# Projecting queries and keys for a later pair among the inner layers instead of among the exponentials, in an attention and feed-forward kernel on one NeuronCore

## The chip, the core and the metric

The kernel runs on one core of one Trainium2 chip. The metric is the time of one execution on the device in microseconds (us), lower is better. The figure shown for the kernel before is the median of three runs. TensorE is called PE here, VectorE DVE, ScalarE ACT, GpSimd POOL and SyncE SP, as in the profile.

## The reference

One transformer layer over 32 sequences of 256 tokens with 128 features, all in float32. Attention has 16 heads of 8 features, a causal mask and a distance penalty on the scores; the feed-forward part has hidden width 512 and weights that are small integers times a scale.

```python
Q, K, V = (split_heads(x @ W.T + b) for W, b in ((Wq, bq), (Wk, bk), (Wv, bv)))
scores = einsum('bhid,bhjd->bhij', Q, K) / sqrt(8)
scores = where(j > i, -inf, scores - (i - j))
attn = softmax(scores) @ V                       # heads joined again
x = layernorm(x + attn @ Wo.T + bo)
h = silu((x @ w1.T) * s1) * ((x @ w2.T) * s2)    # 128 -> 512
h = gelu((h @ h1.T) * sh1)                       # 512 -> 512
h = gelu((h @ h2.T) * sh2)                       # 512 -> 512
x = layernorm(x + (h @ w3.T) * s3)               # 512 -> 128
```

## The kernel before

Two sequences, 512 tokens, make a pair, and 16 pairs (0 to 15) go through the kernel one after the other. The program is a software pipeline, written out by hand: Python generators are advanced one step at a time, and the order in which their steps are called is the order of the instructions on PE, DVE, ACT and SP. The wrapper `InOrder` keeps that order, so that nearly all instructions of these engines carry its line, L58. POOL's instructions have lines of their own.

`step(n)` is iteration n. It has two stages.

**The loop** (L733 to L752) has twelve rounds. In each, `weigh(n, i)` computes one group of transposed scores of pair n on PE (tile `s`, two blocks of 512 columns in PSUM), ACT takes their exponential (`e`), and POOL zeroes what lies above the diagonal (L463). `row_maxima(n + 1, i)` computes the same kind of scores for the next pair, adds the mask with four small products, and DVE reduces them to row maxima (`m`), which that pair's exponentials will subtract. Every third round is a "diagonal" one with smaller blocks (`s_0d` to `s_3d`). Between the rounds stand steps of other work: the second half of pair n-2's last layer (`last`: tiles `pw`, `yT`, `py`, `y`, `z`), the products of exponentials and values (`outputs`: `pa`, `pt`), the transpose of pair n-1's normalized rows (`turn`: `px1T`), and, up to the change, the projection of pair n+2.

**The feed** (L793 to L795) is the feed-forward part of pair n-1: four blocks of the first layer (`pw`, Silu), then four blocks of each inner layer, `podd` and `peven`, with Gelu. The products of an inner layer come in three groups: sixteen for blocks 0 and 1, eight for block 2, eight for block 3. Hidden values are kept as a rounded part and a rest, each multiplied separately, so ACT takes each Gelu twice (`heven`, then `evenw`), and DVE subtracts the one from the other. For the last block of the second inner layer DVE copies instead. `feed` yields twelve times, each time between the products of a block and its activations, and at each yield the generator `rest()` does one step of other work: the last `outputs`, `maxima_to_rows`, `project_values`, the output projection (`finish`: `pon`, `onT`, `po`) and two layer norms. What is left of `rest()` when `feed` ends is run behind it (L795).

**The projection**, `project(n)`, has three steps. The first issues the load of the next pair's `x`, transposes this pair's rows on PE (`pxT`, four transposes), copies them to SBUF on DVE (`xT`) and adds the output bias to `x` on POOL (L325). The second multiplies by the query weights (`pq`), and `halves` writes a rounded part on ACT (`qhi`, Identity) and the rest on DVE (`qlo`). The third does the same for the keys (`pk`, `khi`, `klo`). The tiles qhi, qlo, khi and klo have one buffer each. At the end of the loop `stack(n + 2, ...)` copies them by DMA into the stacked operands `qs` and `ks`.

What sets the order around the change:

- Score tiles `s`, and the layers' `pw`, `podd` and `peven` in the feed, come from one pool of three PSUM buffers (L283); `pxT`, `pq`, `pk` and the other small products share two PSUM buffers of another pool (L284).
- The exponential, Silu and Gelu need different tables on ACT: `prepare` makes ACT load one ahead of its use, three times an iteration. The one for Exp stands at the end of the feed (L616).
- `late` holds the last step of `last(n - 2)`, the second norm's output and its store, and runs in round 3 of the next loop (L738).

Of the kernel before, what the change touches and what calls it, by code (L numbers as in the profile page):

```python
# [42 lines left out]
NPAIR = B // 2  # L43
# [18 lines left out]
def tile_attn_ffn(  # L62
# [39 lines left out]
    def load_x(n):  # L102
        t = xin[n % 4]
        sp.dma_start(out=t, in_=xv[n])
        return t
# [53 lines left out]
    def prepare(func):  # L159

        act.activation(nothing, half[:, 0:1], func)
# [124 lines left out]
    def work(nm):  # L286
        return ps_w.tile([P, 512], F32, name=nm, tag="work")
# [7 lines left out]
    def halves(n, ps, bias, nm):  # L295
        pool = setup if n == 1 else hlp
        hi = pool.tile([P, TOK], F32R, name=f"{nm}hi_{n}", tag=f"{nm}hi")
        act.activation(hi, ps, AF.Identity, bias=bias)
        lo = pool.tile([P, TOK], F32R, name=f"{nm}lo_{n}", tag=f"{nm}lo")
        vec.scalar_tensor_tensor(  # L300
            lo, ps, bias, hi.bitcast(F32), ALU.add, ALU.subtract
        )
        return hi, lo
# [10 lines left out]
    def project(n):  # L314
        xn = xs[n]
        if n + 1 < NPAIR:
            xs[n + 1] = load_x(n + 1)
        pt = work(f"pxT_{n}")
        for t in range(NT):
            pe.transpose(pt[:, t * P : (t + 1) * P], xn[:, t, :], ident)  # L320
        xT = xtp.tile([P, TOK], F32, name=f"xT_{n}", tag="xT", bufs=2)
        vec.tensor_copy(xT, pt)

        for t in range(NT):
            nc.gpsimd.tensor_tensor(xn[:, t, :], xn[:, t, :], bo_sb, ALU.add)  # L325
        yield
        pq = work(f"pq_{n}")
        pe.matmul(pq, lhsT=wq_sb, rhs=xT, start=True, stop=True)
        q = halves(n, pq, bq_sb, "q")
        yield  # L330
        pk = work(f"pk_{n}")
        pe.matmul(pk, lhsT=wk_sb, rhs=xT, start=True, stop=True)
        k = halves(n, pk, bk_sb, "k")
        m = mp.tile([P, 2, 2, H], F32, name=f"m_{n}", tag="m")
        pairs[n] = dict(
            q=qs[n % 2], k=ks[n % 2], qs=q, ks=k, m=m, xT=xT, xb=xs.pop(n)
        )
# [192 lines left out]
    def first_norm(n):  # L530
        x1 = x1s[n % 3]
        yield from layernorm(pairs[n]["xb"], x1, f"a_{n}")
        pairs[n] = dict(x1=x1)
# [4 lines left out]
    def turn(n, exact):  # L538
        pt = work(f"px1T_{n}")
        for t in range(NT):  # L540
            pe.transpose(pt[:, t * P : (t + 1) * P], pairs[n]["x1"][:, t, :], ident)
        x1T = xtp.tile([P, 2, TOK], F32R, name=f"x1T_{n}", tag="x1T")
        if exact:
            act.copy(x1T[:, 0, :], pt)
            vec.tensor_tensor(x1T[:, 1, :], pt, x1T[:, 0, :].bitcast(F32), ALU.subtract)
        else:
            x1T = x1T.bitcast(F32)
            vec.tensor_copy(x1T[:, 0, :], pt)
        pairs[n]["x1T"] = x1T
# [72 lines left out]
    def inexact_weights():  # L622

        found = const.tile([P, 11], F32, name="found")
        at = 0
        for nm, *_ in layers:
            rows = [t[nm].rearrange("p k o -> p (k o)") for t in (loaded, near)]
            for c in range(0, rows[0].shape[1], HID):
                whole, part = (t[:, c : c + HID] for t in rows)
                act.copy(part, whole)  # L630
                differ = once.tile([P, HID], F32, name=f"differ_{at}", tag="differ")
                vec.scalar_tensor_tensor(
                    differ, whole, 1.0, part.bitcast(F32), ALU.mult, ALU.not_equal,
                    accum_out=found[:, at : at + 1],
                )
                at += 1
                yield
        ones_col = const.tile([P, 1], F32, name="ones_col")
        nc.gpsimd.memset(ones_col, 1.0)
        count = work("pcount")  # L640
        pe.matmul(count[0:1, 0:11], lhsT=ones_col, rhs=found, start=True, stop=True)
        total = const.tile([1, 1], F32, name="total")
        vec.tensor_reduce(total, count[0:1, 0:11], AX.X, ALU.add)
        number = const.tile([1, 1], I32, name="number")
        vec.tensor_copy(number, total)
        pairs["inexact"] = number

    def last(n, exact, ws, gp):
        h = pairs[n]["h"]
        pT = work(f"pw3_{n}")  # L650
        for k in range(KC):
            parts = [h[:, i, k, :] for i in range(2 if exact else 1)]
            product(pT, ws["w3"][:, k, :], parts, k == 0, k == KC - 1)
        yT = gp.tile([P, TOK], F32, name=f"yT_{n}", tag="sg")
        act.activation(yT, pT, AF.Copy, scale=sc["s3"])
        yield
        po = work(f"py_{n}").rearrange("p (t d) -> p t d", d=D)
        for t in range(NT):
            pe.transpose(po[:, t, :], yT[:, t * P : (t + 1) * P], ident)
        y = yp.tile([P, NT, D], F32, name=f"y2_{n}", tag="y")  # L660
        z = yp.tile([P, NT, D], F32, name=f"z_{n}", tag="z")
        if n == NPAIR - 1:

            norms = []
            for t in (slice(0, NT // 2), slice(NT // 2, NT)):
                vec.tensor_tensor(y[:, t], po[:, t], pairs[n]["x1"][:, t], ALU.add)
                norms.append(layernorm(y[:, t], z[:, t], f"f_{n}_{t.start}"))
                next(norms[-1])
            for norm, t in zip(norms, (slice(0, NT // 2), slice(NT // 2, NT))):
                run(norm)  # L670
                sp.dma_start(out=ov[n][:, t], in_=z[:, t])
            return
        vec.tensor_tensor(y, po, pairs[n]["x1"], ALU.add)
        yield
        yield from layernorm(y, z, f"f_{n}")
        sp.dma_start(out=ov[n], in_=z)
        del pairs[n]

    def run(gen):
        for _ in gen:  # L680
            pass


    ahead = project(0)
# [7 lines left out]
    ahead = project(1)  # L692
# [32 lines left out]
    def step(n, exact=None, ws=None, hp=None, gp=None):  # L725


        side = iter(())
        settling = (
            last(n - 2, exact, ws, gp) if n > 1 else first_norm(0) if n else inexact_weights()  # L730
        )
        ahead = project(n + 2) if n + 2 < NPAIR else iter(())
        for i in range(3 * G):  # L733
            weigh(n, i)
            j = i + {0: LEAD, 1: -LAG}.get(n, 0)
            if n + 1 < NPAIR and 0 <= j < 3 * G:
                row_maxima(n + 1, j)
            if i == 3 and late:  # L738
                run(late.pop())
            next(side, None)  # L740
            if n and i == 9:
                turn(n - 1, exact)
            if i in ((0, 2) if n > 1 else (0, 2, 4, 6)) if n else i < 11:
                next(settling, None)

            if i in ((3, 4, 5) if n == 1 else (1, 3, 5)):
                next(ahead, None)
            if i % 3 == 2:
                run(side)
                side = outputs(n, i // 3)  # L750
            if n == 0 and i == 3 * G - LEAD:
                maxima_to_rows(1)  # L752
        if n < 2:
            run(settling)
        run(ahead)
        if n + 2 < NPAIR:
            stack(n + 2, "q")
            stack(n + 2, "k", sp if n else act)


        def rest():
            for _ in range(3):
                next(side)
                yield
            if n == 1:
                for i in range(3 * G - LAG, 3 * G):
                    row_maxima(2, i)
                    yield
            if 0 < n < NPAIR - 1:
                maxima_to_rows(n + 1)  # L770
            run(side)
            yield
            if n + 2 < NPAIR:
                project_values(n + 2)
                yield
            last_steps = finish(n)
            next(last_steps)
            yield
            yield from last_steps
            if n:  # L780
                yield
                yield from first_norm(n)
            if n == NPAIR - 1:
                yield
                turn(n, exact)
            if n > 1:
                next(settling)
                late.append(settling)

        if n:  # L790
            prepare(AF.Silu)
        due = rest()
        for _ in feed(n - 1, exact, ws, hp, gp) if n else ():  # L793
            next(due, None)
        run(due)  # L795
# [85 lines left out]
```

## Time and profile before

| | |
|---|---|
| median of 3 runs | 823.32 us (823.05 to 824.74) |
| the profiled execution | 824.06 us, span 822.2 us, granted PE clock 0.98 |
| loop of iteration 6, 318.45 to 341.72 us | 23.27 us |
| feed of iteration 6, 341.72 to 365.86 us | 24.14 us |
| busy share of the span | PE 95%, DVE 77%, ACT 64%, POOL 32% |

The profile is one execution taken by the hardware profiler; its times count from the start of its span. A row names an engine, an operation, its output and inputs by the program's names, and its duration; the time that an engine sat idle ahead of an instruction stands in brackets with what ended it. PE and ACT instructions are pipelined: the next one can start before the last has ended, so work is best measured from start to start. The clock column is the share of full speed that was granted to PE.

### The profile page before, as it was taken

What the parts mean: (1) busy time and instruction counts of PE and PEld (TensorE: products, weight loads), DVE (VectorE), ACT (ScalarE), POOL (GpSimd) and SP (SyncE); (2) the same over time, 40 slices, a digit from 0 to 9 for tenths busy, and PEclk for the clock granted to TensorE, in tenths of its full rate; (3) what the DMA queues carried; (4) which work ended last, traced back from release to release, by engine and by line L of the source; (5) the groups of instructions that cost most, each with busy time, mean ns of one, the idle gap of its engine ahead of it and who ended that gap; (6) DMA issues with size and microseconds to landing.
All of it is one profiled execution on the core that took longest, in us unless ns stands there. A gap on an engine that the chain in (4) does not pass through costs nothing.

```text
span 822.2 us, 17431 instructions
## 1 busy us (share of the span) xinstructions
PE 784.6 (95%) x7046; PEld 555.8 (68%) x7046; DVE 636.0 (77%) x1247; ACT 527.5 (64%) x719; POOL 260.8 (32%) x341
## 2 busy tenths in 40 slices
PE   4896999999999999999999999999999999999994
PEld 2664676776767677676767767676767767666673
DVE  6786778877887887778788877888878787873674
ACT  5065556766666766766576676667666666758572
POOL 5033413333142333414232342424243231424211
PEclk9879999999999999999999999999999999999998
DMA  6824140403204140410404040130404022000001
GB/s 147 213 62 106 29 92 14 106 15 74 60 14 106 28 107 14 92 42 21 110 17 106 27 101 20 43 90 15 107 26 104 4 62 59 14 4 14 1 8 37
DMA packets 39898, 47.49 MB, mean 58 GB/s; under 512 B 3968, under 2 KB 21632, under 8 KB 39808
## 3 DMA queue, kind: packets, MB, share of 16 engines
q1 hardware_dynamic: 37152, 42.82, 22.0%
q10 hardware_dynamic: 2656, 3.48, 1.9%
q8 instruction: 57, 0.93, 0.5%
q14 instruction: 33, 0.27, 0.1%
HBM read 7.48 MB, written 4.19 MB: 14 GB/s over the span
## 4 chain that ended last, share of the span: by engine, by line
PE 83%; DVE 4%; ACT 3%; issue 1%; DMA 0%; POOL 0%; ACTq 0%; POOLq 0%; DVEq 0%
PE peven L58 14%; PE podd L58 14%; PE s L58 12%; PE pa L58 11%; PE pw L58 10%; PE s_2d L58 2%; PE s_3d L58 2%; PE po L58 2%; PE s_0d L58 2%; PE s_1d L58 2%; PE pt L58 2%; PE pv L58 2%; PE pk L58 2%; PE pq L58 2%; PE px1T L58 1%; PE py L58 1%
## 5 line engine op out<-in xcount | busy, mean ns | idle before, releaser
L58 DVE TENSOR_REDUCE m<-s 128x4 f32<-128x1024 f32 x128 | 155.5, 1218 | 14.6 <-PE s L58 13.3
L58 ACT ACTIVATE e<-s 128x1024 f32<-128x1024 f32 x128 | 130.7, 1022 | 44.2 <-PE s L58 34.2
L463 POOL TENSOR_SCALAR_AFFINE_SELECT e<-e 128x512 f32<-128x512 f32 x128 | 82.6, 646 | 218.5 <-ACT e L58 189.3
L58 PE MATMUL podd<-h,h_near 128*128 128x512 f32 x512 | 131.3, 403 | 1.0 <-DVE m L58 0.5
L58 PE MATMUL peven<-hodd,h_near 128*128 128x512 f32 x512 | 122.7, 396 | 0.0
L58 PEld LDWEIGHTS peven<-hodd,h_near 128*128 128x128 f32 x512 | 95.7, 187 | 23.4 <-DVE hodd L58 0.3
L58 PEld LDWEIGHTS podd<-h,h_near 128*128 128x128 f32 x512 | 91.8, 188 | 23.1 <-DVE h L58 3.2
L58 ACT ACTIVATE hodd<-podd,sh 128x512 fp32r<-128x512 f32 x64 | 44.0, 688 | 62.7 <-PE podd L58 62.6
L58 PE MATMUL pw<-x1T,w_near 128*128 128x512 f32 x256 | 75.6, 418 | 1.1 <-DVE h0w L58 1.1
L274 POOL TENSOR_TENSOR rsa<-rsa,half 128x4 f32<-128x4 f32 x16 | 16.3, 1018 | 176.7 <-DVE rsa L58 176.7
L58 DVE SCALAR_TENSOR_TENSOR h0w<-pw,s,sg 128x512 f32<-128x512 f32 x64 | 47.9, 748 | 30.4 <-ACT sg L58 30.4
L58 PEld LDWEIGHTS s<-qs,ks 64*128 64x128 f32 x512 | 38.9, 188 | 47.7 <-issue 34.1
L58 PE MATMUL pa<-e,vaug 128*32 128x256 f32 x1024 | 70.6, 389 | 0.0
L58 PE MATMUL s<-qs,ks 64*128 64x256 f32 x512 | 65.3, 335 | 0.6 <-ACT e L58 0.5
L58 DVE TENSOR_TENSOR heven<-evenw,heven 128x512 fp32r<-128x512 f32 x64 | 44.2, 692 | 26.6 <-ACT evenw L58 26.1
L58 ACT ACT_TABLE_LOAD x47 | 60.3, 1283 | 3.4 <-issue 2.6
L58 ACT ACTIVATE sg<-pw,s 128x512 f32<-128x512 f32 x64 | 43.7, 684 | 28.2 <-PE pw L58 27.9
L58 PE MATMUL s<-ks,qs 62*128 62x256 f32 x512 | 56.9, 302 | 2.4 <-ACT e_0d L58 1.8
L58 ACT ACTIVATE heven<-peven,sh 128x512 fp32r<-128x512 f32 x48 | 33.4, 696 | 39.8 <-PE peven L58 39.8
L58 PEld LDWEIGHTS pw<-x1T,w_near 128*128 128x128 f32 x256 | 43.4, 188 | 18.4 <-ACT nothing L58 5.8
L581 POOL TENSOR_TENSOR h<-h0w,h 128x512 fp32r<-128x512 f32 x31 | 40.0, 1291 | 43.5 <-DVE h L58 41.2
L58 DVE TENSOR_TENSOR hodd<-oddw,hodd 128x512 fp32r<-128x512 f32 x64 | 43.7, 684 | 10.0 <-ACT oddw L58 9.9
(147 smaller groups left out, 1418.1 us busy)
## 6 DMA issues: line engine op xcount, KB each, us to landing
qs<-qhi SPq DMA_DIRECT2D x32, 256.0 KB
qs<-qlo SPq DMA_DIRECT2D x32, 256.0 KB
ks<-khi SPq DMA_DIRECT2D x26, 256.0 KB
ks<-klo SPq DMA_DIRECT2D x26, 256.0 KB
x<-in_x_dram SPq DMA_DIRECT2D x16, 256.0 KB
out_dram<-z SPq DMA_DIRECT2D x15, 256.0 KB
ks<-khi ACTq DMA_DIRECT2D x6, 256.0 KB
ks<-klo ACTq DMA_DIRECT2D x6, 256.0 KB
```

The source lines that it names most:

```text
L58: return lambda *args, **kw: self.tc.keep_in_program_order(call(*args, **kw))
L274: nc.gpsimd.tensor_tensor(rs, rs, half[:, 0:NT], ALU.pow)
L463: nc.gpsimd.affine_select(out=on_diagonal, in_=on_diagonal, pattern=[[0, on_diagonal.shape[1]], [1, P]], base=0, channel_multiplier=-1, co ...
L581: (nc.gpsimd if o < (1 if final else 2) else vec).tensor_tensor(h[:, 1, o, :], whole, h[:, 0, o, :].bitcast(F32), ALU.subtract)
```

## The change

Pairs 0 to 3 are projected as before. For pairs 4 to 15 the three steps of the projection move out of the loop of iteration n (where pair n+2 was projected, in rounds 1, 3 and 5) and into the end of the feed of the iteration before: in `rest()` of iteration n, pair n+3 is projected. From iteration 2 to 12 the first step falls to the tenth yield of the feed, the second to the eleventh, none to the twelfth, and the third behind the feed. In iteration 1, where `rest()` is three steps longer, all three fall behind the feed. The loops of iterations 2 to 13 hold no projection any more. The stacking copies stay at the end of the loops.

```diff
@@ in step(n), ahead of the loop
-        ahead = project(n + 2) if n + 2 < NPAIR else iter(())
+        ahead = project(n + 2) if n < 2 else iter(())
@@ in rest()
         def rest():
+            later = project(n + 3)
             for _ in range(3):
                 next(side)
                 yield
...
             if n > 1:
                 next(settling)
                 late.append(settling)
+            if 0 < n < NPAIR - 3:
+
+                yield
+                for _ in range(2):
+                    next(later)
+                    yield
+                yield
+                run(later)
```

## The prediction

> **What bounds the kernel now.** I read the page first: busy time by engine, then the chain that ended last.
>
> ```profile
> span 822.2 us, 17431 instructions
> ...
> PE 784.6 (95%) x7046; PEld 555.8 (68%) x7046; DVE 636.0 (77%) x1247; ACT 527.5 (64%) x719; POOL 260.8 (32%) x341
> ...
> PE 83%; DVE 4%; ACT 3%; issue 1%; DMA 0%; POOL 0%; ACTq 0%; POOLq 0%; DVEq 0%
> ```
>
> TensorE (PE) is the bound, but an average hides stages. So I split the time by windows: the twelve score rounds of iteration 6 ("the loop"), the layers behind them ("the feed"), and the loop of iteration 14, where no pair is left to project.
>
> ```profile
> core 0: us, PE busy (x) PEld busy (x) DVE busy (x) ACT busy (x) POOL busy (x), PEclk, DMA share, GB/s
> ...
> 318.45:341.72 23.27, 23.27 (x301) 15.65 (x300) 19.90 (x26) 16.48 (x20) 9.99 (x15) 1.00 0.05 13
> ...
> 341.72:365.86 24.14, 24.14 (x144) 18.23 (x141) 18.44 (x50) 15.72 (x25) 5.71 (x5) 1.00 0.45 102
> ...
> 697.62:718.95 21.33, 21.03 (x293) 14.77 (x293) 17.85 (x23) 15.22 (x18) 8.38 (x11) 1.00 0.05 14
> ```
>
> In iteration 6 PE is busy for the whole of both stages, 23.27 + 24.14 = 47.41 us. The other starts of iterations 2 to 14 lie the same 47.4 us apart. The third row matters most: it is a loop of the old kernel without projections, which is what the change makes of loops 2 to 13. In iteration 6's chain pxT, pq and pk take 0.59, 1.05 and 1.05 us, 2.69 together. Without them the loop should last 23.27 - 2.69 = 20.58 us. It lasts 21.33. The chain of waits in that window tells where 0.75 us went:
>
> ```profile
> 697.73 0.69 ACT evenw L58
> ...
> 698.43 1.28 ACT L58
> ...
> 699.93 0.91 ACT e L58
> 700.85 0.58 ACT yT L58
> 701.42 0.92 ACT e L58
> 702.35 0.04 issue
> 702.39 0.92 PE s_0d L58 x12
> ...
> 707.31 1.15 DVE m L58
> 708.46 0.04 issue
> 708.50 1.10 PE s L58 x12
> ```
>
> Scores of weigh and of row_maxima take turns in three PSUM buffers. So the maxima's scores of round i+1 wait for the exponential of round i, and weigh's of round i+2 for the reduction of round i. At 702.39 PE waits for the second exponential (its eight products before started at 701.51 and take 0.50: 0.38 lost), at 708.50 for a reduction; smaller delays follow such waits. In iteration 6 the transposes pxT and product pq fill these moments: PE reaches the place later and waits for nothing.
>
> **The change, part by part.** Twelve pairs, 4 to 15, are projected one iteration earlier. In the built order of the changed kernel, iterations 2 to 12 put pxT behind the first sixteen products of the second inner layer (peven), pq behind the next eight, and pk behind the last eight, ahead of the next loop's first scores ("the seam"). In iteration 1, whose rest is three steps longer, all three stand at the seam in a row.
>
> *PE work* is conserved but for neighbours: four transposes take 0.59 us between scores and 0.44 among layer products (rows pxT and pon). pq and pk are 1.05 in either place, by the row. Saved: 12 x 0.15 = 1.8 us.
>
> *Loops 2 to 13 lose their filler.* Nearest row: iteration 14, +0.75 us. One delay goes: the second maxima's scores now start 0.44 before their mask, where 0.33 is usual, because the first exponential has just ended; pk ahead of them moves that apart. I take 0.75 - 0.11 = 0.64 us, x 12 = 7.7 us. Bounds: 0 (all waits absorbed) and 0.95, 0.2 above the row, for the queues that follow.
>
> *The seam's new queueing.* khi now stands between the table load and the first exponential, klo ahead of the first reduction. Counted from the seam with iteration 6's steps: khi starts at 2.22, the exponential at 2.80 and ends at 3.82; PE wants its buffer at 1.05 + 0.86 + 2.06 + 0.34 = 4.31. Covered. klo starts at 2.95, the reduction 0.67 later, at 3.62, and ends at 4.84; PE wants that buffer at 4.82. Break-even: each 0.1 us more here would cost 1.2 us over twelve loops. The second exponential follows yT, which needs the last layer's products (end 4.04): yT 4.08, exponential 4.65 to 5.67, while PE is there at 5.32. So the wait of iteration 14 stays, about 0.4. What is late next is that same exponential, so the reduction's margin costs nothing by itself.
>
> *pq waits for xT in the feed.* DVE copies xT behind the subtraction for the first block of the layer, which itself waits for ScalarE's second Gelu. Two lines of the timeline show it: DVE in iteration 6's feed, and PE in iteration 1's, where a transpose, its copy and the product behind it stand in a row:
>
> ```profile
> 363.53 0.69 DVE L58 TENSOR_TENSOR heven<-evenw,heven 128x512 fp32r<-128x512 f32 x1 [0.75 <-ACT evenw L58]
> ...
> 124.10 1.16 PE L58 MATMUL po<-wo_sb,onT 128*128 128x128 f32 x8 [0.79 <-DVE onT L58]
> ```
>
> peven starts at 358.30 and takes 0.233 a product: sixteen end at 362.03, pxT at 362.47, eight more at 364.34. DVE starts xT 0.60 after 363.53, at 364.13; it lasts 0.68 and PE may go on 0.05 later (708.45 to 708.50), at 364.86. Wait 0.52 us, x 11 = 5.7 us. Bounds: 0.11, what po loses in iteration 6 behind eight covering products (355.43 instead of 355.32), and 0.79, the second line above, where nothing covers such a copy. I keep 0.52, as its queue is walked with this stage's own rows. Queued behind pq are the last eight peven products; all that follows shifts with them.
>
> *Iteration 1.* pxT, copy and pq are back to back at the seam, and the copy stands behind the last subtraction on DVE (130.55, next start 131.16, seam 128.92). Copy 2.24 to 2.92 after the seam, pq at 2.97; PE was free at 0.45. Wait 2.5 us, once; at least 0.79, the po row.
>
> *At nothing.* qhi on ACT waits for pq and holds up the third Gelu pair, but that pair ends as the last block's products do (both near 3.5 us behind pq's start); if not, 0.1 us each time. No row shows a table load for these Identity activations beside Exp, and the built order has none beside Gelu. The four bias adds on POOL (1.74 us) now stand ahead of the second norm's power (1.01 us), needed only by z some 10 us later. On SP the x load keeps its place behind the maxima's copies and waits for the same norm (361.58). The stacking copies (341.19 to 347.40) stay where they are, and free qhi and qlo some 17 us before their new writers.
>
> Sum: 7.7 + 5.7 + 2.5 - 1.8 = +14.1 us. The profiled execution took 824.06, 0.74 above the median of the runs, 823.32, and would become 838.2 with a span of 836.3; from the median, 837.4.
>
> *Rules of the skill.* In iteration 14's loop PE waits, and its granted clock is 1.00. The Trainium skill, "TensorE: Matmul & The Clock Gate", section "A second HAM failure mode: psum-queue depth-cycling", says that frequent small idles between matmul groups while PSUM buffers are cycled can throttle the clock. At half the clock a 21 us loop would lose some 20 us, an estimate from that page's two states; that speaks against the change, but the row does not show it, and the sum leaves it out. The loop has DVE at 19.90 of 23.27 us, the feed at 18.44 of 24.14. "Perfetto Trace Analysis", section "Optimization Strategy", advises interleaving regimes whose busiest engine differs, which moving DVE work to the feed would serve; here PE is full in both, so the rows leave no gain from it.
>
> **Rivals.** *PE's work alone counts:* if xT were ready in time and the loops waited for nothing, PE would save 1.8 us of transposes and 12 x 0.11 of the exponential's delay, 3.1 us, and lose only the 0.8 of iteration 1's floor: 821.0. It decides if pq's wait and the lost fill stay under 0.2 us an iteration together (2.3 / 12). PE's 95% speaks for it; iteration 14 against. *Copy hidden, loops waiting:* if DVE reached xT 0.5 us earlier, 14.1 - 5.7 = +8.4: 831.7. The subtraction's place ahead of it speaks against. *The seam on the path:* if klo and khi delay the first reduction's buffer by 0.4 more than walked, 12 x 0.4 on top: 842.2. The break-even margin speaks for it, the later exponential wait against. *The change not done* is out: the built order shows twelve pairs moved.
>
> **How the numbers follow.** Forecast 0.62, copy hidden 0.15, seam 0.13, PE alone 0.10. About 0.2% (1.6 us) can be told from no change. Of the last case 0.06 is faster and 0.04 the same; the other three are slower: 0.90. The range, 829 to 842, holds the forecast, the hidden copy with loop waits a third smaller (831.7 - 2.6), and nearly all of the seam case.
>
> **What would show it.** Right: pitch 48.4 instead of 47.4 us; loops of 21.2 us plus pk; pq with 0.4 to 0.6 us of idle on DVE's xT eleven times and 2.5 once; PE idle on ACT's e about 0.4 a loop; PE busy about 2 us less. Wrong: a pitch of 47.2 with PE full in loops 2 to 13 would end the fill argument; a pq without idle would end the copy's term; a granted clock under 1.00 in these loops would bring in a cost that I left out.

## The result, and the profile after

The changed kernel took 838.38 us (median of four runs, 837.74 to 838.84), the kernel before 823.45 beside it: 1.0175 times as long, 95% interval 1.0159 to 1.0192, 14.9 us more. Its profiled execution has a span of 836.9 us. The forecast was 837.4 with a span of 836.3.

The page, first the busy times, then the chain that ended last by engine:

```profile
span 836.9 us, 17409 instructions
...
PE 788.0 (94%) x7046; PEld 557.5 (67%) x7046; DVE 637.6 (76%) x1247; ACT 530.1 (63%) x719; POOL 265.8 (32%) x341
...
PE 63%; DVE 15%; ACT 9%; issue 4%; DMA 1%; POOL 0%; SPq 0%; ACTq 0%; POOLq 0%; DVEq 0%
```

Every engine issues as many working instructions as before, and the chain tells the difference: PE carried 83% of it before, now 63%, and DVE and ACT carry 24% instead of 7%. PE now waits for them again and again. The windows of two stretches behind the end of iteration 1's feed, then of iteration 6's loop behind pk:

```profile
core 0: us, PE busy (x) PEld busy (x) DVE busy (x) ACT busy (x) POOL busy (x), PEclk, DMA share, GB/s
129.43:133.20 3.77, 0.59 (x5) 0.35 (x3) 3.70 (x8) 2.17 (x3) 1.89 (x5) 1.00 0.14 37
133.20:136.20 3.00, 2.98 (x6) 0.85 (x6) 0.75 (x1) 0.69 (x1) 0.00 (x0) 0.64 0.14 44
...
329.35:350.58 21.23, 20.96 (x294) 14.73 (x293) 17.82 (x23) 15.32 (x18) 8.36 (x11) 1.00 0.05 14
```

A loop without a projection lasts 21.23 us, as forecast (21.22), 0.65 more than its work. The stretch from 129.43 was forecast to be idle for 2.5 us; it is idle for 3.2, and the clock behind it is 0.64. Next PE's timeline around iteration 6's loop and feed; the bracket is the idle time ahead and what ended it:

```profile
333.35 0.66 PE L58 MATMUL s_0d<-qs,ks 64*128 64x128 f32 x8 [0.17 <-DVE m L58]
334.03 0.66 PE L58 MATMUL s_0d<-ks,qs 62*128 62x128 f32 x8
...
367.17 3.90 PE L58 MATMUL peven<-hodd,h_near 128*128 128x512 f32 x16
370.90 0.60 PE L58 MATMUL pxT<-ident,x 128*128 128x128 f32 x4
371.25 2.12 PE L58 MATMUL peven<-hodd,h_near 128*128 128x512 f32 x8
373.75 1.13 PE L58 MATMUL pq<-xT,wq_sb 128*128 128x512 f32 x2 [0.39 <-DVE xT L58]
374.32 2.43 PE L58 MATMUL peven<-hodd,h_near 128*128 128x512 f32 x8
376.58 1.02 PE L58 MATMUL pk<-xT,wk_sb 128*128 128x512 f32 x2
377.53 0.50 PE L58 MATMUL s<-qs,ks 64*128 64x256 f32 x4
```

The same places in the kernel before, where pxT stands in round 1 and the feed holds only its own products:

```profile
322.35 0.66 PE L58 MATMUL pxT<-ident,x 128*128 128x128 f32 x4
322.93 0.66 PE L58 MATMUL s_0d<-qs,ks 64*128 64x128 f32 x8
323.43 0.61 PE L58 MATMUL s_0d<-ks,qs 62*128 62x128 f32 x8
...
358.30 7.63 PE L58 MATMUL peven<-hodd,h_near 128*128 128x512 f32 x32
365.86 0.51 PE L58 MATMUL s<-qs,ks 64*128 64x256 f32 x4
```

In round 2 of the changed kernel PE waits 0.17 us for the first reduction, then reaches the next scores at 333.85 and starts them at 334.03, when the second exponential has ended (ACT, 332.96 + 1.02). In the feed PE is through eight products at 373.12, if each takes 0.233 (371.25 + 8 x 0.233), and starts pq at 373.75: 0.63 us, of which the bracket shows the part behind the last product's modelled end. In a run below in which nothing waits there (the transposes one yield sooner), the same eight products take 1.95 us from their start to pq's, not 1.86, because the first of them comes slower behind the transposes; by that row the wait is 0.55 us. On DVE the copy stands where the forecast put it, 0.62 behind the first block's subtraction:

```profile
372.40 0.70 DVE L58 TENSOR_TENSOR heven<-evenw,heven 128x512 fp32r<-128x512 f32 x1 [0.66 <-ACT evenw L58]
373.02 0.68 DVE L58 COPY xT<-pxT 128x512 f32<-128x512 f32 x1
```

Where the span's 14.7 us lie, from the starts of the iterations' first scores in both traces: 0.5 before iteration 1 ends its layers, where the two programs hold the same instructions on PE (that point lies anywhere from 128.4 to 130.9 us in the profiles below, changed or not); 6.75 from there to the first scores of iteration 2; 1.28 up to those of iteration 3; 8.0 in the next ten (48.17 us each instead of 47.39, one of 48.42); then -2.0 where loop 13 is lighter and no feed has to pay for it; 0.2 in the rest.

### The profile page after: what moved, and what is told of

Same layout as the page of the kernel before. It is cut to its first block, busy times and chain, and to the rows that moved or that the text cites. A ratio compares the mean times of both kernels' runs of the same rounds, so it can differ in the third digit from the quotient of the medians.

```text
span 836.9 us, 17409 instructions
## 1 busy us (share of the span) xinstructions
PE 788.0 (94%) x7046; PEld 557.5 (67%) x7046; DVE 637.6 (76%) x1247; ACT 530.1 (63%) x719; POOL 265.8 (32%) x341
## 4 chain that ended last, share of the span: by engine, by line
PE 63%; DVE 15%; ACT 9%; issue 4%; DMA 1%; POOL 0%; SPq 0%; ACTq 0%; POOLq 0%; DVEq 0%
PE podd L58 13%; PE pa L58 9%; PE peven L58 9%; PE pw L58 7%; PE s L58 7%; DVE m L58 6%; PE s_0d L58 2%; ACT L58 2%; ACT evenw L58 2%; PE s_2d L58 2%; PE s_3d L58 2%; PE po L58 2%; PE pq L58 2%; PE pt L58 2%; PE pv L58 2%
## 5 line engine op out<-in xcount | busy, mean ns | idle before, releaser
L58 PE MATMUL peven<-hodd,h_near 128*128 128x512 f32 x512 | 131.5, 406 | 0.0
L58 DVE TENSOR_TENSOR heven<-evenw,heven 128x512 fp32r<-128x512 f32 x64 | 44.1, 690 | 19.8 <-ACT evenw L58 19.3
```

The lines of the kernel that those rows point to most:

```text
L58: return lambda *args, **kw: self.tc.keep_in_program_order(call(*args, **kw))
```

## The experiments

Theory A is the prediction's: three separate costs, namely fill that the loops lose (exponentials and reductions then release the three PSUM buffers too late), pq's wait for xT, and the stack of steps at iteration 1's seam. Rival B puts the loops' cost on khi and klo, which now stand ahead of the first exponential and the first reduction. Rival C denies iteration 1 a cost of its own, rival D says that waits only change places. All edits are of the changed kernel unless told otherwise.

**pq behind the layers.**

```diff
                 yield
-                for _ in range(2):
-                    next(later)
-                    yield
+                next(later)
+                yield
+                yield
                 yield
                 run(later)
```

> From the changed kernel (838.4 us): pq moves from between the last two groups of peven to the seam, ahead of pk, so sixteen products instead of eight lie between pxT and pq. Theory A (pq's wait for xT is one cost, lost fill in the loops the other): the 0.63 us wait of eleven iterations goes, nothing else changes, because the first exponential (now behind qhi and khi, ending 4.4 us behind the seam) still ends before PE wants its buffer at 5.2: 838.4 - 6.9 = 831.5. Rival B (what the loops lose comes from khi and klo standing ahead of the first exponential and the first reduction): a second pair of them there adds up to 0.58 us a loop and eats the gain: about 838.

Measured: 844.14 us, 1.0249 of the kernel before (1.0234 to 1.0265). Neither theory gave that. PE's timeline at iteration 6's seam:

```profile
328.28 1.02 PE L58 MATMUL pq<-xT,wq_sb 128*128 128x512 f32 x2
329.14 1.02 PE L58 MATMUL pk<-xT,wk_sb 128*128 128x512 f32 x2
...
332.10 2.13 PE L58 MATMUL pw<-heven,w_near 128*128 128x512 f32 x8 [1.09 <-DVE qlo L58]
```

pq's wait is gone, as A said, but the next product waits 1.1 us for `qlo`. The pool of small products has two PSUM buffers: pxT and pk use one, pq and `pw` the other, so `pw` may start only when qlo has read pq. qlo follows qhi, and qhi now stands behind the table load for Exp on ACT (330.59). The pitch went from 48.17 to 48.69 us. The expectation had left this pool out.

**Pair 4 in the loop again.**

```diff
-        ahead = project(n + 2) if n < 2 else iter(())
+        ahead = project(n + 2) if n < 3 else iter(())
-            if 0 < n < NPAIR - 3:
+            if 1 < n < NPAIR - 3:
```

> From the changed kernel: pair 4 alone is projected in the loop of iteration 2 again, so iteration 1 has no projection at its seam. Theory A: the 6.75 us between the end of iteration 1's layers and the first scores go (wait 3.2 us, then products at a lower granted clock), and loop 2 takes 23.3 us again instead of 21.8: 838.4 - 5.2 = 833.2, with the clock back at 1.00 there. Rival C (iteration 1 costs what any other does): 838.4 - 0.8 = 837.6.

Measured: 832.87 us, ratio 1.0108 (1.0092 to 1.0123). A's figure; rival C falls. One pair of twelve cost over a third of the slowdown. PE is busy in all of 130 to 153 us there, with a granted clock of 1.00.

**px1T into round 1.**

```diff
-            if n and i == 9:
+            if n and i == (1 if n > 1 else 9):
                 turn(n - 1, exact)
```

> From the changed kernel: the four transposes px1T, 0.59 us of PE work that the loop has anyway, move from round 9 to round 1 in iterations 2 to 15, into the place that pxT left. Theory A: PE reaches the round's second scores later and waits for neither the first reduction nor the second exponential, and less at round 6; 0.5 to 0.6 us a loop, 13 loops: 838.4 - 7 = 831. Rival B (the late start of exponentials and reductions at the seam is what costs): the queue on ACT and DVE is no shorter, px1T's own copies join it: 838 to 839.

Measured: 831.51 us, ratio 1.0101 (1.0085 to 1.0118), pitch 47.70. No work was added or taken away, and ACT and DVE have as much ahead of their first exponential and reduction as in the changed kernel. PE's timeline of the round, with no bracket left:

```profile
330.02 0.66 PE L58 MATMUL px1T<-ident,x 128*128 128x128 f32 x4
330.61 0.66 PE L58 MATMUL s_0d<-qs,ks 64*128 64x128 f32 x8
331.11 0.61 PE L58 MATMUL s_0d<-ks,qs 62*128 62x128 f32 x8
```

Four transposes in the place that pxT had left gave back 0.47 us an iteration. Rival B does not explain that. (In this execution the clock stayed at 1.00 in iteration 1, and the stretch from pxT to the next scores took 5.70 us instead of 6.75, though PE waited the same 3.19.)

**One part alone: only the transposes in the feed.** pq and pk stay in rounds 3 and 5 of the loops.

```diff
@@ in rest()
-                for _ in range(2):
-                    next(later)
-                    yield
-                yield
-                run(later)
+                next(later)
+                begun[n + 3] = later
@@ in step(n)
-        ahead = project(n + 2) if n < 2 else iter(())
+        ahead = project(n + 2) if n < 2 else begun.pop(n + 2, iter(()))
```

> One part alone, from the kernel before (823.4 us): only the first step of the projection (transposes, xT, bias adds, the load) moves to the feed; pq and pk stay in rounds 3 and 5 of the loops. Theory A: the feed gains 0.35 us and waits for nothing, the loop loses 0.59 of fill and gets about 0.45 of waits in round 2 back; +0.2 a pair, 12 pairs: 826. Rival B (khi and klo at the seam cost): nothing is at the seam here, the cheaper transposes save 0.24 a pair: 820.6.

Measured: 827.63 us, ratio 1.0048 (1.0034 to 1.0062); A is right in the sign and low by 1.6 us. Nothing of the projection is at the seam here, and yet the loop waits in round 2:

```profile
324.57 0.66 PE L58 MATMUL s_0d<-qs,ks 64*128 64x128 f32 x8
325.44 0.66 PE L58 MATMUL s_0d<-ks,qs 62*128 62x128 f32 x8 [0.21 <-ACT e L58]
```

The second scores could start at 325.07 and start at 325.44: 0.37 us from having no pxT in round 1. That is the lost fill without any of rival B's causes; rival B expected 820.6.

**Bias adds later, in the program's text.** `project`'s four adds on POOL were written behind its third step.

> From the changed kernel: the four bias adds on POOL leave the projection's first step and follow its last. In iteration 1 they ran beside DVE's norm (1.56 us instead of 1.11) and copy (0.69 instead of 0.42). If POOL's work slows DVE there, both take their old times, xT ends 0.7 us sooner behind the seam and pq's wait falls from 3.2 to about 2.5 us; if they are slow for another reason, nothing of it moves. The total falls by 0.7 us in the one case, to 837.7 (by up to 2.4 if the clock stays up too), and stays at 838.4 in the other; the profile tells, not the time.

Measured: 838.40 us (one run). The edit did not do what it was to do: POOL has nothing ahead of these adds and waits only for the transposes, so they still ran at 129.31 us, and norm and cast took 1.56 and 0.69 as before. It answers nothing.

**Bias adds really later.** They go to round 1 of the next loop, with POOL's order kept there.

```diff
@@ in step(n), round i
+            if i == 1 and 1 < n < NPAIR - 2:
+                add_bias(pairs[n + 2]["xb"], True)
```

> The question that the run before could not answer, since POOL waits only for the transposes and ran its adds as early as ever: here the bias adds of pairs 4 to 15 really stand in round 1 of the next loop, behind the second exponential's mask. If POOL's adds slow DVE in iteration 1, its norm takes 1.11 us again and its cast 0.42, xT ends 0.7 us sooner and pq waits 2.5 us instead of 3.2; 837.7, or 836 where the clock stays up. If they do not, norm and cast stay at 1.56 and 0.69 and the time at 838.4.

Measured: 836.72 us, ratio 1.0163 (1.0145 to 1.018). The time decides nothing, as the changed kernel itself took 837.03 us beside it; the timelines do. Iteration 1 on DVE and then pq on PE, here and in the changed kernel:

```profile
130.01 1.11 DVE L58 TENSOR_SCALAR x<-x,mva,rsa 128x128 f32<-128x128 f32 x4
131.04 0.41 DVE L58 CAST heven<-evenw 128x512 fp32r<-128x512 f32 x1
...
132.83 1.13 PE L58 MATMUL pq<-xT,wq_sb 128*128 128x512 f32 x2 [2.47 <-DVE xT L58]
```

```profile
129.67 1.56 DVE L58 TENSOR_SCALAR x<-x,mva,rsa 128x128 f32<-128x128 f32 x4
131.15 0.69 DVE L58 CAST heven<-evenw 128x512 fp32r<-128x512 f32 x1
...
133.22 1.33 PE L58 MATMUL pq<-xT,wq_sb 128*128 128x512 f32 x2 [3.19 <-DVE xT L58]
```

Without POOL's adds beside them, norm and cast are as fast as before the change (1.11 and 0.42 us at 129.07 and 130.10 there), and pq waits 2.47 us instead of 3.19. So POOL's work beside DVE's did slow it. The Trainium skill, "Perfetto Trace Analysis", section "Optimizing Scalar/DVE Operations", says that the two share a read port of SBUF, which fits; no run here shows the port itself. Not all DVE work suffers: in iteration 6's feed of the changed kernel the subtraction at 372.40 us keeps its 0.70 us beside an add, and there the four adds take longer, 2.17 us instead of 1.77.

**The changed kernel once more.**

> The changed kernel once more, for the clock behind iteration 1's wait: if the wait of 3.2 us is what lowers it, some executions show the lower clock there and some do not (three of four so far), with 0.7 to 1.7 us between them, and no other loop shows it. 838.4 within 1.

Measured: 837.03 us (836.48 to 838.65), ratio 1.0162 (1.0145 to 1.018). The clock behind iteration 1's wait fell again (0.54 from 135 to 138 us), and in no other loop, so it has fallen in four of five executions. The median is 1.4 us below the first one of the same kernel, more than the 1 us expected; a difference of that size between two runs here tells nothing.

**The transposes one yield sooner.**

```diff
-                yield
-                for _ in range(2):
-                    next(later)
-                    yield
+                next(later)
+                yield
+                yield
+                next(later)
+                yield
                 yield
                 run(later)
```

> From the changed kernel: the projection's first step falls to the ninth yield instead of the tenth, the second stays at the eleventh. PE's order is the same from iteration 2 on, but xT stands ahead of the first block's subtraction on DVE, not behind it. Theory A (the copy's queue on DVE is what pq waits for): xT ends 1.3 us sooner, pq's wait of 0.63 goes in eleven iterations, 6.9 us; in iteration 1 the copy comes ahead of the last block's cast and subtraction, 1.5 to 3.5 us. 838.4 - 8.4 to 10.4 = 828 to 830. Rival D (the wait only changes place again, as qlo's did when pq went behind): 835 to 839.

Measured: 827.96 us, ratio 1.0052 (1.0036 to 1.0068), pitch 47.51. DVE copies xT ahead of the first subtraction, behind the norm's statistics, and PE runs through:

```profile
367.46 0.68 DVE L58 COPY xT<-pxT 128x512 f32<-128x512 f32 x1
368.20 0.70 DVE L58 TENSOR_TENSOR heven<-evenw,heven 128x512 fp32r<-128x512 f32 x1
```

```profile
367.06 2.11 PE L58 MATMUL peven<-hodd,h_near 128*128 128x512 f32 x8
369.01 1.02 PE L58 MATMUL pq<-xT,wq_sb 128*128 128x512 f32 x2
369.46 2.42 PE L58 MATMUL peven<-hodd,h_near 128*128 128x512 f32 x8
```

The pitch fell by 0.66. From the start of the eight products to pq's start it is 1.95 us instead of 2.50, which is the wait of 0.55, and from there to the next products' start 0.45 instead of 0.57. In iteration 1 pq waits 1.86 us, and the clock stays up. Rival D falls: a wait moved in the first experiment because a buffer was in use, not because it must.

**All three, and z later.** Pair 4 in the loop, px1T in round 1, transposes sooner; then also `late` in round 7 instead of 3.

> From the changed kernel: pair 4 in the loop of iteration 2, px1T in round 1, transposes at the ninth yield. If the three costs are separate, their gains add: 5.5 + 6.9 + 6.9 = 19.3 us, 819.1, 0.5% under the kernel before. If one cover serves two of them, 822 to 826.

> The same, and the second norm's output z of the pair before in round 7 instead of round 3. The reduction that round 6's scores wait for then no longer stands behind z on DVE: the 0.15 us that PE waits there goes in 13 loops, 2 us, 817. If exponentials and not reductions release round 6, no change against the run without it.

Measured: 819.09 us, ratio 0.9944 (0.9926 to 0.9962), and 819.57 us, ratio 0.994 (0.9917 to 0.9962). The first is what separate gains add up to (838.4 - 19.3 = 819.1; its pitch, 47.04 us, is 48.17 - 0.47 - 0.66), and it is faster than both kernels, by 0.56% against the one before. z later brings nothing. In round 6 the first scores start sooner after their predecessor (0.24 instead of 0.39 us behind the mask's start), so a reduction did hold them, and the second give it back: 0.57 behind the first instead of 0.42. The second wait for the exponential of round 5 in both cases.

## Why the prediction was right

It named the right costs in the right places: the lost fill, pq's wait and iteration 1's stack were each confirmed by an edit that took one of them away. That the sum came so near, +14.7 us of span for +14.1, is luck as well: errors of two to four us cancel in it.

- *Lost fill:* forecast 0.64 us a loop, measured 0.65. The nearest row, a loop of the old kernel without projections, was worth more than any walk. One detail of the seam was off: the first reduction's margin did cost something (0.17 us), but it only took from the second exponential's wait, as the step had said of the sum.
- *pq's wait:* forecast 0.52, measured 0.55 against the run without a wait (0.63 if the eight products are counted at 0.233 each). Its cause was confirmed where the copy moved on DVE and PE's order stayed. The 0.44 for pxT held too, if the 0.09 by which the product behind it comes slower is counted with its 0.35; the lower bound of 0.11, read from po, was for the most part this same slower start and not a wait.
- *PE's work:* the mis-sized term. The step let pq and pk cost 1.05 us in either place and saved 0.15 a pair. From the second layer's start to the first scores PE now takes 10.36 us instead of 7.56; less the wait of 0.55 that is 2.25 for the projection, where it took 2.69 among the scores. The saving is 0.44 a pair (0.52 with the wait at 0.63), some 3 to 4 us more over the eleven iterations than forecast. pq was 0.96 and pk 0.95 between layer products.
- *Iteration 1:* forecast 2.5 us of wait, measured 3.2, plus a lower clock behind it: from pxT to the first scores 6.75 us instead of the 5.07 that the step adds up to (0.45 + 2.52 + 2 x 1.05), and half a us more in loop 2, 2.2 us in all. The bias adds, costed at nothing by their own queue, slowed DVE beside them by 0.7 us; with them moved the wait was 2.47.
- *Start:* 0.5 us of the difference lies ahead of iteration 1's end, where nothing was changed on PE, and is chance.
- *Signs:* pitch 48.17 instead of 48.4; PE busy rose by 3.4 us instead of falling by 2. Busy time misled here: in iteration 6 PE is busy for 47.53 of 48.18 us, 0.65 idle, though its waits by the starts of products add up to about 1.2, because modelled ends reach into the waits; and products at a low clock count as more work.
- *Clock:* in the loops it stays 1.00 with all their small waits, as the row had it. What the one long wait would do to it the prediction left out.

## What to carry to other kernels

Work that fills an engine's waits costs less than its duration where it stands; look for a place in the trace where it is already absent before costing its removal at full price. Another filler in the same place can give the time back (0.47 of the 0.65 us here, with four transposes that compute something else), so moving work out of a saturated stage goes with choosing what takes its place. When a consumer is given more distance from its producer, follow every ring of buffers that both share, the short one of two above all.

## What the runs showed of the hardware

Behind PE's idle stretch of 3.2 us in iteration 1 the granted clock fell to 0.50 for 3.4 us (134.01 to 137.42 us in the changed kernel's profile) in four of five profiled executions, and not at all in the fifth, which has the same instructions up to there; it stayed at 1.00 behind 2.47 and 1.86 us, one execution each. The Trainium skill, "TensorE: Matmul & The Clock Gate", section "HAM oscillation — how this bites in real kernels", puts the limit at idle gaps of about 3.4 us; here 3.2 us were enough in most executions. pk took up to 1.85 us there instead of 0.95.

The place of the idle stretch in time may decide, and not its length alone. Within each trace all changes of the granted clock lie whole multiples of 3.413 us apart; on that grid, continued to iteration 1, the four executions had 2.6 to 3.1 us of idle in one step, the fifth 1.8 at most, and those with the shorter waits 1.9 and 1.7. No run moved the stretch alone, so this is not shown. It gives no threshold either: in the first 84 us of these programs 0.50 also followed steps with 1.7 to 2.0 us of idle.

The same four transposes take 0.58 us of PE among scores of 62 and 64 rows and 0.35 among layer products, and fp32 products of 128 by 512 take 1.05 and 0.96 a pair: in these traces what an operation costs on PE depends on what stands on either side of it.
